# Sharing the band loads of a fused convolution and involution between two DMA queues

## The chip, the cores and the metric

The kernel runs on one core of a Trainium2 chip. Its engines work side by side, each through its own list of instructions in order: TensorE (PE in the profile) multiplies matrices into PSUM, VectorE (DVE) and ScalarE (ACT) do elementwise work, GpSimd (POOL) and SyncE (SP) here issue nearly all transfers. Engines wait for each other through semaphores. The metric is the device time of one execution in microseconds (us); lower is better.

## The reference

The input x has 32 images of 256 channels and 32 x 32 pixels. Two residual layers follow each other. `_gn` is a group norm over 32 groups of 8 channels.

```python
# layer 0: a 3x3 convolution, 256 to 256 channels, values clipped to the range of a 16-bit float
x = x + _L0_conv_ref(_gn(x), L0_conv_weight, L0_conv_bias)
# layer 1: an involution; n is _gn(x)
y = relu(batchnorm(einsum('oc,bchw->bohw', w1, n)))            # 256 -> 64 channels
w = einsum('oc,bchw->bohw', w2, y) + b2                        # 64 -> 16 groups x 49 taps, for each pixel
patches = [pad(n)[:, :, i:i+56, j:j+56] for the 49 taps]       # here 32 for 56
x = x + einsum('bgkhw,bgckhw->bgchw', w, patches)              # each pixel has its own 7x7 kernel for each group
```

In the second layer, each pixel thus has its own weights: 49 taps for each of 16 groups, shared by the 16 channels of a group.

## The kernel before

All images go through one software pipeline, written out by hand: the loop at lines 532 to 574 runs over steps, 16 per image, and in each step appends a few instructions for several images at once. `due(n, lag)` tells which image and which of its 16 steps stand at that point for a given lag. The order of a list of instructions of an engine is the order in which these calls are made. Nothing is reordered later.

For an image the work goes as follows.

- `front` (L272) normalizes x, runs the convolution (L318, tile `pc`), adds it to x (L334), normalizes again into `xn`, forms y (L366, L373) and the transposed pixels (L381, L385). It starts 58 steps ahead of the image's sums. x itself is loaded by SyncE (`load_x`, L103) 63 steps ahead, into one of five tiles; a tile is free when the image that held it has been stored.
- `weights` (L388) makes the per-pixel weights of four image rows with TensorE (L396, tile `pw`), and VectorE writes them with bias into the tile `w_sb` (L414). This tile is a ring of 24 image rows, which is three bands of eight rows. A slot may be overwritten when the scatter that read it has landed. It runs 18 steps ahead.
- `scatter` (L452) writes the weights of a band to a tensor `wd` in the chip's HBM memory, with seven transfers of SyncE (L463), 160 KB each. The rearrangement between weights per pixel and weights per tap lies in the addresses of this write and of the read that follows.
- `load_bands` (L465) reads a band of eight rows back into one of three band tiles. It takes 16 transfers, each of which fills 8 of the 128 partitions with 8 x 2 rows of 4496 bytes. All of them are issued by GpSimd (L475). A band has to wait for its scatter, and for TensorE to have finished with the band three before it.
- `sums` (L486) multiplies a band with the pixels (L500, tile `acc`), twice per band, and `add_windows` (L508) adds the result to x (L516). `store` (L518) sends half an image out by SyncE (L521).

There are four bands per image, so 128 bands, 2048 band loads and 896 scatters in an execution. `scatter` of band k+1 comes at the same step as, and in the list ahead of, `load_bands` of band k, for most k; the two stores, the load of x for a later image and the first scatter of the next follow at an image's end.

The tile framework gives the transfers of each kind of queue eight semaphores in turn: eight for GpSimd's queue and eight for the others. A transfer waits for the one eight before it on the same set. So eight of GpSimd's transfers and eight of SyncE's can be under way. GpSimd does nothing else in the body than issue band loads.

Of the kernel before, what the change touches and what calls it, by code (L numbers as in the profile page):

```python
# [40 lines left out]
JC = W // SIDES  # L41
# [9 lines left out]
WB = G * WIN  # L51
WPIX = K1 * WB + XR
# [6 lines left out]
ROW = S * WPIX  # L59
WR = 4  # L60
NBAND = 3
NPIX = 6
RING = 24
FRONT = -58
# [5 lines left out]
def tile_quant_conv_then_involution(  # L70
# [16 lines left out]
    nc = tc.nc  # L87
# [56 lines left out]
    y_sb = [const.tile([P, N // 2], F32, name=f"y_{i}") for i in range(2)]  # L144
    bands = [const.tile([P, SIDES, WINC * WB + XR], F32, name=f"band_{i}") for i in range(NBAND)]
    for t in bands[CH:]:
        nc.gpsimd.memset(t, 0.0)
    pixels = [const.tile([P, 2, PAIRS, PAIR], F32, name=f"pixels_{i}") for i in range(NPIX)]
    for t in pixels:
# [41 lines left out]
    for col, cols, at, n in (  # L191
# [8 lines left out]
        )  # L200
        nc.sync.dma_start(to, bands[NBAND - 1][:H, 0, :n].unsqueeze(1).to_broadcast([H, cols, n]))

# [69 lines left out]
    def front(b):  # L272
# [103 lines left out]
        for m in range(0, M, 2):  # L376
            yield
            pt = ps_m.tile([P, 2, C], F32, tag="m", name="pt")
            for i in range(2):
                for h in range(CH):  # L380
                    nc.tensor.transpose(  # L381
                        pt[:, i, h * P : (h + 1) * P], xn[:, h, (m + i) * P : (m + i + 1) * P], ident
                    )
            to = pixels[(b * M + m) // 2 % NPIX].rearrange("p i a (v c) -> p (i a) v c", c=GC)
            nc.scalar.copy(to[:, :, ::2], pt.rearrange("p i (a v c) -> p (i a) v c", v=2, c=GC))  # L385
# [79 lines left out]
    def load_bands(b, k):  # L465

        band = bands[(b * K + k) % NBAND]
        for i in range(JC):
            j = i // 2 + i % 2 * JC // 2
            src = bass.AP(  # L470
                tensor=wd.tensor,
                offset=wd.offset + k * TR * ROW + (j + PAD1) * WPIX,
                ap=[[ROW - 1, TR], [JC * WPIX, SIDES], [1, WPIX]],
            )
            nc.gpsimd.dma_start(band[j::JC, :, j * WB : j * WB + WPIX], src)  # L475

    def windows(b, m):

# [7 lines left out]
    def sums(b, m):  # L486

        k, d = divmod(m, SIDES)
        j0 = 0 if d else PAD1
        band = bands[(b * K + k) % NBAND][:, d]  # L490
        px = pixels[(b * K + k) % NPIX][:, d]
        for h in range(CH):
# [34 lines left out]
    def due(n, lag):  # L527

        b, i = divmod(n - lag, per)
        return (b, i) if 0 <= b < B else (None, None)  # L530

    with tc.manual_schedule():
        fronts = {}
        for n in range(FRONT, B * per + 2):
            b, i = due(n, FRONT)
# [10 lines left out]
            b, i = due(n, 0)  # L546
            if b is not None and i % 2 == 0:
                sums(b, i // 2)
            b, i = due(n, 1)
# [6 lines left out]
            b, i = due(n, 2)  # L556
            if b is not None and i == 2 * (M - 1 - SIDES):
                store(b, 0)
            b, i = due(n, -LEAD)
# [3 lines left out]
            b, i = due(n, -LEAD + 1)  # L563
# [4 lines left out]
            b, i = due(n, LOAD)  # L568
            if i == 0 and b > 0:
                x_tiles[b] = load_x(b)  # L570

            b, i = due(n, 3 - 4 * NBAND)
            if b is not None and i % 4 == 0:
                load_bands(b, i // 4)
# [37 lines left out]
```

## Time and profile before

| what | value |
|---|---|
| time, median of 3 runs | 1547.64 us (1541.66 to 1551.72) |
| profiled execution | 1520.43 us, span 1518.7 us |
| TensorE busy | 1317.0 us, 87% |
| GpSimd busy | 1141.8 us, 75% |
| VectorE busy | 865.6 us, 57% |
| ScalarE busy | 741.9 us, 49% |
| moved by DMA | 369.36 MB, 243 GB/s in the mean |
| GpSimd's queue (q0) | 147.59 MB, 35.7% of the 16 engines' span |
| SyncE's queue (q1) | 217.29 MB, 48.7% |
| band load, issue to landing | median 4.6 us |
| scatter transfer, issue to landing | median 5.4 us |

Busy shares are means over a start of about 80 us in which no bands are loaded, a long body, and a tail of some 110 us in which no new image comes in. A queue's share of the DMA engines is the time that its packets took, divided by sixteen times the span. An engine's idle time is listed by what ended it, with the total, the number of times and the longest one.

### The profile page before, as it was taken

Reading aid. Unit: us, or ns where it says so; the run is one execution under the profiler, and the core shown is the slowest. Engines: PE = TensorE matmul, PEld = TensorE weight load, DVE = VectorE, ACT = ScalarE, POOL = GpSimd, SP = SyncE. Lnnn points to the kernel's source line nnn. Section 1 sums busy time; section 2 is a strip of 40 time slices with the busy share of each in tenths; the row PEclk is TensorE's granted clock in tenths of the full one; section 3 lists DMA queues with packets and bytes.
Section 4 is the critical chain, followed back from the end, with each engine's and each line's share of the span. In section 5 each row is a group of like instructions: output and inputs, shape, how many; then the busy total and the mean of one; then the engine's idle time right before and its main releaser. Section 6 shows DMA issues by size and latency. Waiting matters only on the chain.

```text
span 1518.7 us, 70106 instructions
## 1 busy us (share of the span) xinstructions
PE 1317.0 (87%) x29760; PEld 865.2 (57%) x29760; DVE 865.6 (57%) x2764; ACT 741.9 (49%) x1699; POOL 1141.8 (75%) x2068
## 2 busy tenths in 40 slices
PE   5899989989998988989989898998989887998664
PEld 2456656656566555656656565665656565665543
DVE  4356656656665654656656565565656555665442
ACT  5665545435555544555545455554545554553200
POOL 6068787778777787877877777778777787788786
PEclk9899999999999999999999999999999999999877
DMA  6088998988998898898989898989989888988885
GB/s 198 5 232 248 265 256 254 270 255 243 267 252 246 257 270 258 236 273 240 258 245 272 247 259 241 258 259 255 280 248 264 239 251 238 272 250 238 250 232 149
DMA packets 372375, 369.36 MB, mean 243 GB/s; under 512 B 84768, under 2 KB 314336, under 8 KB 371808
## 3 DMA queue, kind: packets, MB, share of 16 engines
q1 hardware_dynamic: 273760, 217.29, 48.7%
q0 software_dynamic: 98304, 147.59, 35.7%
q8 instruction: 236, 3.87, 1.0%
q14 instruction: 75, 0.61, 0.1%
HBM read 183.81 MB, written 180.74 MB: 240 GB/s over the span
## 4 chain that ended last, share of the span: by engine, by line
PE 43%; DMA 29%; POOL 12%; issue 7%; DVE 4%; ACT 3%; SPq 2%; POOLq 0%; DVEq 0%; ACTq 0%
DMA band<-wd 24%; PE pc L318 17%; PE acc L500 13%; POOL band L475 12%; PE pw L396 8%; DMA wd<-w_sb 5%; DVE w_sb L414 2%; PE pt L381 2%; PE py L366 2%; SPq L463 2%; PE pg L221 1%; ACT junk L213 1%; ACT y L373 1%; DVE x L516 1%; DVE w_sb L154 0%
## 5 line engine op out<-in xcount | busy, mean ns | idle before, releaser
L475 POOL DMA_DIRECT2D band<-wd x2048 | 1117.1, 548 | 362.8 <-DMA band<-wd 218.1
L414 DVE TENSOR_TENSOR w_sb<-pw,b_sb 128x16 f32<-128x16 f32 (+9 forms) x1920 | 453.8, 349 | 569.7 <-PE pw L396 567.8
L318 PE MATMUL pc<-xq,wq 128*128 128x496 f16 (+3 forms) x2304 | 543.5, 383 | 11.3 <-ACT xq L266 5.9
L500 PE MATMUL acc<-band,pixels 64*32 64x190 f32 (+1 forms) x16384 | 420.7, 327 | 93.6 <-DMA band<-wd 78.8
L500 PEld LDWEIGHTS acc<-band,pixels 64*32 64x32 f32 x16384 | 306.1, 109 | 165.4 <-issue 93.5
L318 PEld LDWEIGHTS <-wq 128*128 128x128 f16 x2304 | 208.7, 99 | 312.5 <-issue 111.0
L396 PE MATMUL pw<-w_sb,y 64*32 64x224 f32 (+1 forms) x8192 | 295.8, 337 | 23.4 <-issue 22.7
L516 DVE TENSOR_TENSOR x<-acc,x 128x380 f32<-128x380 f32 (+1 forms) x512 | 263.4, 515 | 39.2 <-PE acc L500 30.2
L396 PEld LDWEIGHTS pw<-w_sb,y 64*32 64x32 f32 x8192 | 186.9, 108 | 50.0 <-issue 35.6
L213 ACT ACTIVATE junk<-x 128x512 f16<-128x512 f32 (+1 forms) x192 | 148.0, 771 | 137.3 <-DVE r L244 120.0
L385 ACT COPY pixels<-pt 128x512 f32<-128x512 f32 x128 | 74.4, 581 | 244.3 <-PE pt L381 244.3
L213 ACT ACTIVATE junk<-x,mean 128x1024 f16<-128x1024 f32 x128 | 147.1, 1149 | 4.1
L381 PE MATMUL pt<-ident,xn 128*128 128x128 f32 x512 | 81.1, 281 | 25.3 <-ACT ve L240 15.2
L332 DVE TENSOR_SCALAR q<-pc 128x512 f16<-128x512 f32 x128 | 87.3, 682 | 25.1 <-PE pc L318 25.1
L266 ACT ACTIVATE xn<-x,off,rstd 128x512 f32<-128x512 f32 x128 | 96.1, 799 | 0.0
L334 DVE SCALAR_TENSOR_TENSOR x<-q,bias_sb,x 128x512 f32<-128x512 f16 x128 | 91.9, 718 | 0.4
L221 PEld LDWEIGHTS pg<-sums,avg 128*128 128x128 f32 x320 | 54.0, 194 | 56.5 <-ACT y L373 30.6
L381 PEld LDWEIGHTS pt<-ident,xn 128*128 128x128 f32 x512 | 59.0, 142 | 44.2 <-ACT ve L240 18.3
L266 ACT ACTIVATE xq<-x,off,rstd 128x1024 f16<-128x1024 f32 x64 | 78.6, 1233 | 9.0 <-PE pc L318 8.4
L221 PE MATMUL pg<-sums,avg 128*128 128x2 f32 x320 | 47.6, 232 | 37.5 <-ACT y L373 22.0
L228 ACT ACTIVATE mean<-pg 128x2 f32<-128x2 f32 x64 | 11.0, 171 | 133.6 <-PE pg L221 133.6
L366 PEld LDWEIGHTS py<-xn,w_sb 128*64 128x64 f32 x2048 | 64.8, 142 | 19.6 <-issue 9.3
(39 smaller groups left out, 375.7 us busy)
## 6 DMA issues: line engine op xcount, KB each, us to landing
band<-wd POOLq DMA_DIRECT2D x2048, 70.2 KB, 4.6
wd<-w_sb SPq DMA_DIRECT2D x896, 160.0 KB, 5.4
x<-in_x SPq DMA_DIRECT2D x64, 512.0 KB, 5.9
out<-x SPq DMA_DIRECT2D x64, 512.0 KB, 6.3
band<-in_w SPq DMA_DIRECT2D x2, 1152.0 KB, 8.2
w_sb<-in_w SPq DMA_DIRECT2D x2, 196.0 KB, 9.8
wd<-band SPq DMA_DIRECT2D x2, 180.0 KB, 3.9
b_sb<-in_b SPq DMA_DIRECT2D x7, 14.0 KB, 8.0
```

The source lines that it names most:

```text
L213: nc.scalar.activation(junk[:, n0:n1], src[:, h, n0:n1], func, bias=bias, accum_out=self.sums[:, part, h : h + 1])
L221: nc.tensor.matmul(pg[:, :CH], avg, self.sums[:, i, :], start=i == 0, stop=i == self.parts - 1)
L266: nc.scalar.activation(dst, src, AF.Identity, bias=self.off[:, one], scale=self.rstd[:, one])
L318: nc.tensor.matmul(pc.rearrange("p (r c) -> p r c", c=W)[:, r0 - nt * RT : r1 - nt * RT, c0:c1], wq[:, kh, k, mh * P : (mh + 1) * P], xq[: ...
L334: nc.vector.scalar_tensor_tensor(xt[:, mh, cols], q, bias_sb[:, mh : mh + 1], xt[:, mh, cols], ALU.add, ALU.add)
L366: nc.tensor.matmul(py[i * CR : (i + 1) * CR, cols], w1_sb[:, kh, :], px[:, r : r + 2], start=kh == 0, stop=kh == CH - 1,)
L381: nc.tensor.transpose(pt[:, i, h * P : (h + 1) * P], xn[:, h, (m + i) * P : (m + i + 1) * P], ident)
L396: nc.tensor.matmul(pws[i][t * TW : (t + 1) * TW, r, : dj.stop - dj.start], y_sb[b % 2][half, (r0 // 2 + r) * W : (r0 // 2 + r + 1) * W], w ...
L414: nc.vector.tensor_tensor(to, pws[i][:p, r : r + rows, e, d0 * G : d1 * G].rearrange("p r (d g) -> p r d g", g=G), b2_sb[:p, e, d0 * G : d ...
L475: nc.gpsimd.dma_start(band[j::JC, :, j * WB : j * WB + WPIX], src)
L500: nc.tensor.matmul(at[t * TW : (t + 1) * TW, h, :, f - top : l - top], px[p, a, v * GC : v * GC + TW], of[:, :, 2 * a + v, f - top : l - top],
L516: nc.vector.tensor_tensor(x_at, of, x_at, ALU.add)
```

## The change

Of the 16 transfers of a band, the fourth, eighth, twelfth and sixteenth are issued by SyncE, the other twelve by GpSimd as before. What is loaded, from where and to where stays as it is. It is meant to take issue work off GpSimd, using a queue that exists already.

```diff
 WR = 4
 NBAND = 3
+SHARE = 4
 NPIX = 6
...
                 ap=[[ROW - 1, TR], [JC * WPIX, SIDES], [1, WPIX]],
             )
-            nc.gpsimd.dma_start(band[j::JC, :, j * WB : j * WB + WPIX], src)
+            queue = nc.sync if i % SHARE == SHARE - 1 else nc.gpsimd
+            queue.dma_start(band[j::JC, :, j * WB : j * WB + WPIX], src)
```

In the changed program SyncE's list per image holds 28 scatters, 2 stores, 2 loads of x and 16 band loads, in the order: seven scatters of band k+1, four loads of band k. One store stands ahead of the last of an image's four scatter groups and the other right behind it; four band loads follow that second store, and the two loads of x come after them. TensorE's first matmul of a band now waits for twelve semaphores of transfers where it waited for eight.

## The prediction

> **What bounds the kernel now.** I read the chain of waits on the page first, since it says which work follows which to the end, then the costliest groups, then who waits for whom, and last the stages.
>
> ```profile
> PE 43%; DMA 29%; POOL 12%; issue 7%; DVE 4%; ACT 3%; SPq 2%; POOLq 0%; DVEq 0%; ACTq 0%
> DMA band<-wd 24%; PE pc L318 17%; PE acc L500 13%; POOL band L475 12%; PE pw L396 8%; DMA wd<-w_sb 5%; DVE w_sb L414 2%; PE pt L381 2%; PE py L366 2%; SPq L463 2%; PE pg L221 1%; ACT junk L213 1%; ACT y L373 1%; DVE x L516 1%; DVE w_sb L154 0%
> ```
>
> The band loads hold 24% + 12% = 36% of the chain, in flight or being issued. TensorE holds 43%, so there are two streams of nearly equal weight. The groups show what a load costs its issuer:
>
> ```profile
> L475 POOL DMA_DIRECT2D band<-wd x2048 | 1117.1, 548 | 362.8 <-DMA band<-wd 218.1
> L500 PE MATMUL acc<-band,pixels 64*32 64x190 f32 (+1 forms) x16384 | 420.7, 327 | 93.6 <-DMA band<-wd 78.8
> ```
>
> GpSimd issues 2048 loads at 548 ns, 1117 us. Who waits for whom:
>
> ```profile
> POOL band L475 <- DMA band<-wd: 218.1, 271, 3.2
> POOL band L475 <- DMA wd<-w_sb: 72.9, 31, 56.1
> POOL band L475 <- issue: 52.9, 70, 3.3
> POOL band L475 <- PE acc L500: 2.1, 6, 0.5
> PE acc L500 <- DMA band<-wd: 78.8, 42, 5.5
> PE pw L396 <- issue: 22.7, 13, 4.1
> ```
>
> GpSimd waits 218 us for its own loads: each load waits for the one eight before it. It waits for TensorE to free a band for only 2 us, and for scattered weights for 73 us, 56 of them before the first image. So from 83 us to 1506 us (1423 us) GpSimd is busy (1117) or held by its own loads (218) or by small issue gaps (53): 1388 us, 98%. It is a full queue. The landings in the trace agree: over images 3 to 28 the first L500 matmul of a band follows the band's last landing by 0.1 us in the median for the first of an image's four bands, and its first load starts 4.9 to 12.5 us after the band buffer was free. Bands arrive just in time.
>
> ```profile
> 110.00:1403.00 1293.00, 1168.38 (x26987) 769.50 (x26970) 770.04 (x2496) 661.07 (x1518) 1006.97 (x1847) 0.98 0.90 255
> 1403.00:1485.00 82.00, 52.51 (x1498) 40.78 (x1505) 38.24 (x139) 12.27 (x26) 66.28 (x123) 0.82 0.86 242
> 1485.00:1519.00 34.00, 14.95 (x432) 11.05 (x422) 8.28 (x16) 0.00 (x0) 20.06 (x37) 0.75 0.44 126
> ```
>
> In these stages (columns: length, busy PE, PEld, DVE, ACT, POOL, clock, DMA share, GB/s) TensorE is 90% busy until 1403 us, and only 67 of 116 us after that, when no new image feeds it. So the loads cost little in the body and much in the tail. Gaps of TensorE over 1 us that end at L500 add up to about 42 us after 1403 us; the other 37 or so of the 79 lie in the body, 1.2 us per image of 44.3 us.
>
> **What the Trainium skill says.** "DMA: Bandwidth & Descriptors", section "Issuing engines are not separate DMA queues": transfers of all issuers run on the same 16 DMA engines and interleave; several issuers save only issue time. Here issue time is what is full, 98% of GpSimd, and the two queues do share engines at a DMA share of 0.90, so I expect issue relief and no bandwidth. The same page, section "Why a DMA increments its semaphore by 16 and not by 1": a transfer uses the largest number up to 16 of engines that divides the slowest dimension of both sides, and a hardware queue takes the lowest-numbered ones, while GpSimd's goes round. A load here has 8 partitions and 8 rows, hence 8 engines, always the same half on SyncE's queue. No run so far shows that.
>
> **The change part by part.**
> *GpSimd.* 16 of 64 loads per image leave it: 512 x 0.548 = 281 us of issue, and with them about a quarter of the 218 us, some 54 us. A band needs 12 x 0.548 = 6.6 us plus about 1.3 us of waits, 8 us, against 8.8 + 2.1 = 10.9 now and a pace of 44.3 / 4 = 11.1 us. GpSimd stops being full; it will wait for scattered weights and freed bands instead, which come 4 to 12 us before it uses them now.
> *SyncE, cost of a load.* Its issue of this shape isn't in the trace. Nearest rows: the scatter of L463 at 302 ns at least, 678 median, 2247 at most, and the x load at about 0.53 us. I take 0.75 us, because the four stand right behind seven scatters; ends 0.3 and 1.5. 512 x 0.75 = 384 us, 12 per image.
> *SyncE, room.* Its own waits:
>
> ```profile
> SPq L463 <- DVE w_sb L414: 434.6, 122, 49.6
> SPq L103 <- DMA out<-x: 146.8, 27, 8.6
> SPq L463 <- DVE x L516: 57.5, 98, 2.0
> ```
>
> All its waits are near 700 us, 650 of them in the body: 20 us per image, so 12 us fit. 4.6 us of the 20 is the x load waiting for a store to land; by the order of the changed program four loads stand between that store and the x load, so these 3 us are hidden.
> *Waits added and what is queued behind.* The order on SyncE becomes: scatter of band k+1, loads of band k, with stores and x loads between. The loads wait for TensorE to free the band, which the scatter just ahead implies, since its weights come later in TensorE's order; I put that at nothing. They also share eight slots with the scatters. Behind the loads stand the next scatter, two stores and the x load. Following one image in the trace (690 to 736 us), SyncE idles 7.2, 3.5, 0.6 and 0.1 us ahead of the four scatters. Four loads (3 us) fit before the first two, and push the other two, a store and the x load by 2 to 4 us. Who feels it: VectorE, which overwrites a slot of w_sb once its scatter has landed. That slack, from landing to L414, is 0.2 to 9.1 us, median 4.3, for an image's first band, the late one, and median 5.4 or more for the others. And ScalarE, whose first read of x comes a median of about 5 us after landing. A delay of 3 us is mostly absorbed; I charge 0.3 us per image, 10 us, and 3 us for x.
> *TensorE.* Its wait for a band names 12 semaphores for 8: two more EVENT_SEMAPHORE of about 0.1 us each with the gap behind it, 128 x 0.2 = 26 us if exposed. When the band is early they run beside pc matmuls of L318 (as at 700 us), so I take 5.
> *Landing.* Same bytes, same engines: 0 for the mean. In packets the page gives band loads 35.7% of 16 engines; a quarter, 8.9 points, doubled on one half of the engines, makes 85.5 + 8.9 = 94% there and 77% on the other. Those shares count queueing: the median 4496-byte packet takes 174 ns, the mean 246, so true load is lower and I take no loss, with 0 to 60 us as bounds.
>
> **Sum.** Body: of 37 us of waits I recover 34. Tail: a band takes 9.2 us there; 12 loads make 7 us, and TensorE's 67 us in 12 bands are 5.6, so of 42 us about 28 come back. 62 - 10 - 3 - 5 = 44 us. 1547.6 - 44 = 1503.
>
> **Rivals.**
> 1. *TensorE's floor is reached*: all 79 + 4 us of band waits go and nothing new comes. For it: SyncE's 20 us of room. Against: the small slack of w_sb. 1548 - 83 = 1465; earlier bands don't help ScalarE's share of the waits. Chance 0.2.
> 2. *SyncE's queue takes the wait over*: scatters 4 to 5 us late, so that VectorE, then pw (L396), stall 2 us per image, 62 us, which cancels the gain: 1548. For it: L396 already has 23 us of gaps, at 333 us one of 4.1 us, with a scatter in flight for 8.2 us. Against: the slack above. Chance 0.11.
> 3. *Slower*: half of the DMA engines fill up, scatters land 6 us late and stall VectorE for 3 us per image: 93 + 18 - 62 = 49 us net, 1597; or with 1.5 us per load SyncE needs 24 us where 20 are free, some 2 us beyond what the x wait hides, 62 - 28 = 34 us more, 1582. For it: DMA share 0.90. Against: 243 GB/s are moved as before. Chance 0.12.
>
> **How the numbers follow.** My forecast, 1503, has 0.57. It spreads from 1490 to 1530, since the charges of 18 us may be as small as 4 or as large as 44, and all of that is faster by over 1% (below 1532). With rival 1 faster has 0.77, same 0.11 (rival 2), slower 0.12 (rival 3). The range goes from 1462, just under rival 1, to 1560, past rival 2, and leaves rival 3 out.
>
> **What will show it.** GpSimd: 1536 loads, about 841 us busy, waits that name wd<-w_sb or acc more than before. L500's wait for band<-wd under 35 us. The chain led by TensorE, with band loads under 20%. SyncE: waits for w_sb down from 435 to under 250 us. The last three bands closer than 9 us each. Wrong, if L396's gaps grow past 60 us, if SyncE's loads take over 1.2 us, or if scatters land over 8 us after issue in the median (5.4 now).

## The result and the profile after

The changed kernel takes 1481.45 us in the median of 4 runs (1477.42 to 1488.62); the kernel before took 1544.65 us beside it (1536.92 to 1551.72). The ratio is 0.9596, with a 95% interval of 0.9555 to 0.9638: about 63 us or 4% less. The forecast was 1503 us.

The kernel before runs at different speeds on different chips: on the four chips of the experiments below its median lies between 1522 and 1549 us, and its profile shown ahead is of an execution of 1520 us. Runs on different chips are therefore compared by their ratio to the kernel before on the same chip, and steps within the two profiles add up to 42 us (1518.7 to 1476.7 us), not to 63. Ratios use fast executions alone, which leaves out two of the four of e6 and one of the kernel before beside e1 to e4, and the time given for e6 is the median of its other two. Lines move by one or two in the changed file: L475 became L477, L500 L502, L463 L464, L414 L415, L396 L397.

The chain of waits on the page of the changed kernel, by engine and by line:

```profile
DMA 37%; PE 37%; SPq 9%; DVE 6%; POOL 5%; issue 4%; ACT 2%; DVEq 0%; POOLq 0%; ACTq 0%
DMA band<-wd 20%; DMA wd<-w_sb 16%; PE pc L319 14%; PE acc L502 12%; SPq L464 7%; PE pw L397 7%; POOL band L477 5%; DVE w_sb L415 3%; PE pt L382 2%; SPq L477 1%; DMA out<-x 1%; DVE x L518 1%; PE py L367 1%; ACT junk L214 1%; PE pg L222 1%
```

GpSimd's issue of loads has gone from 12% of the chain to 5%. But TensorE doesn't lead it. The scatters (wd<-w_sb) have risen from 5% to 16%, and SyncE's issue of them from 2% to 7%. The waits between engines say the same (columns: us in total, times, longest):

```profile
POOL band L477 <- DMA band<-wd: 399.1, 279, 9.3
POOL band L477 <- DMA wd<-w_sb: 112.5, 24, 54.5
...
DVE w_sb L415 <- DMA wd<-w_sb: 72.9, 20, 6.9
ACT junk L214 <- DMA x<-in_x: 65.4, 45, 3.0
...
DVE w_sb L415 <- DMA band<-wd: 36.5, 9, 6.3
...
PE acc L502 <- DMA band<-wd: 22.1, 29, 5.1
...
PE pw L397 <- DVE w_sb L415: 18.7, 25, 3.0
...
PE pw L397 <- issue: 17.0, 19, 2.5
```

The two that were next to nothing before, from the same view of the kernel before:

```profile
ACT junk L213 <- DMA x<-in_x: 4.3, 4, 2.5
...
DVE w_sb L414 <- DMA wd<-w_sb: 1.9, 1, 1.9
```

TensorE's wait for bands fell from 79 to 22 us. Two waits are new: VectorE waits for transfers before it may overwrite w_sb, 73 + 36 us where it was 1.9, and ScalarE waits for x, 65 us where it was 4.3. The 399 us of GpSimd look worse than the 218 before and aren't. Taken apart by the place in the band, GpSimd's gaps ahead of the first load of a band grew from 29 to 331 us, and the gaps ahead of all others fell from 273 to 210. It now waits to be allowed to begin. A band's first load waits for semaphores on which SyncE's scatters and SyncE's loads both count, so 226 of these 331 us stand under band<-wd. Its own full slots hold it less than before.

SyncE's own waits, those of over 20 us:

```profile
SPq L464 <- DVE w_sb L415: 71.9, 25, 47.9
SPq L104 <- DMA out<-x: 57.5, 27, 3.5
SPq L477 <- DMA wd<-w_sb: 31.4, 45, 1.9
SPq L477 <- DMA x<-in_x: 23.0, 21, 2.4
SPq L523 <- DVE x L518: 20.4, 16, 7.5
```

SyncE waited 435 us for weights before, and 72 us now, 48 of them before the first scatter. When it comes to a scatter, the weights have been ready for some time. In the trace, from the end of the last L415 that a scatter group stands behind to its first scatter, the medians of the four bands of an image are 5.6, 4.8, 2.1 and 4.4 us (images 3 to 28; negative numbers below mean a start shortly before that end). Before the change the scatter started at once (0.1 us at most). Between 200 and 1250 us SyncE issues transfers for 80% of the time, 55% before.

The stages of the changed kernel (length, busy PE, PEld, DVE, ACT, POOL, clock, DMA share, GB/s), cut to match those of before:

```profile
110.00:1363.00 1253.00, 1153.32 (x26718) 753.14 (x26721) 761.79 (x2474) 656.22 (x1513) 752.23 (x1375) 1.00 0.94 260
1363.00:1443.00 80.00, 60.48 (x1696) 41.11 (x1688) 45.57 (x157) 13.92 (x30) 52.48 (x96) 0.87 0.92 255
1443.00:1477.00 34.00, 17.08 (x495) 12.86 (x479) 8.38 (x16) 0.00 (x0) 15.29 (x28) 0.70 0.70 205
```

TensorE is 92% busy in the body (90% before), GpSimd 60% (78%). Measured by the first L502 matmul of each band, an image takes 43.71 us over the first 28 images where it took 44.54, 23 us in all. The 15 band steps after that take 9.51 us each where they took 10.58, 16 us in all. About 1.5 us come from an earlier start, and 1.3 us from what follows the last band's first matmul.

Not all of this is shorter waiting. Of the 42 us between the profiles, 37 are idle time of TensorE (201.7 us before, 164.7 after) and 5 are busy time (1317.0 and 1312.0 us). L318 and L500 together were busy for 964.2 us before and for 948.5 after, L396 for 295.8 and 300.0, and the granted clock in the body was 0.98 before and 1.00 after. Whether the clock is higher because TensorE waits less, or differs by itself between these executions, no run separates.

### The profile page after: what moved, and what is told of

The parts are those of the page before. It is cut to its first block, busy times and chain, and to the rows that moved or that the text cites. A ratio compares the mean times of both kernels' runs of the same rounds, so it can differ in the third digit from the quotient of the medians.

```text
span 1476.7 us, 70463 instructions
## 1 busy us (share of the span) xinstructions
PE 1312.0 (89%) x29760; PEld 850.6 (58%) x29760; DVE 865.6 (59%) x2764; ACT 738.7 (50%) x1699; POOL 865.1 (59%) x1556
## 3 DMA queue, kind: packets, MB, share of 16 engines
q0 software_dynamic: 73728, 110.69, 28.2%
## 4 chain that ended last, share of the span: by engine, by line
DMA 37%; PE 37%; SPq 9%; DVE 6%; POOL 5%; issue 4%; ACT 2%; DVEq 0%; POOLq 0%; ACTq 0%
DMA band<-wd 20%; DMA wd<-w_sb 16%; PE pc L319 14%; PE acc L502 12%; SPq L464 7%; PE pw L397 7%; POOL band L477 5%; DVE w_sb L415 3%; PE pt L382 2%; SPq L477 1%; DMA out<-x 1%; DVE x L518 1%; PE py L367 1%; ACT junk L214 1%; PE pg L222 1%
## 5 line engine op out<-in xcount | busy, mean ns | idle before, releaser
L477 POOL DMA_DIRECT2D band<-wd x1536 | 840.4, 549 | 599.2 <-DMA band<-wd 399.1
L415 DVE TENSOR_TENSOR w_sb<-pw,b_sb 128x16 f32<-128x16 f32 (+9 forms) x1920 | 455.6, 350 | 536.5 <-PE pw L397 427.0
L319 PE MATMUL pc<-xq,wq 128*128 128x496 f16 (+3 forms) x2304 | 537.7, 380 | 10.1 <-ACT xq L267 6.0
L502 PE MATMUL acc<-band,pixels 64*32 64x190 f32 (+1 forms) x16384 | 410.8, 321 | 45.5 <-DMA band<-wd 22.1
L502 PEld LDWEIGHTS acc<-band,pixels 64*32 64x32 f32 x16384 | 296.9, 107 | 118.9 <-issue 86.0
L397 PE MATMUL pw<-w_sb,y 64*32 64x224 f32 (+1 forms) x8192 | 300.0, 334 | 36.4 <-DVE w_sb L415 18.7
L397 PEld LDWEIGHTS pw<-w_sb,y 64*32 64x32 f32 x8192 | 181.2, 107 | 74.8 <-issue 50.7
L222 PEld LDWEIGHTS pg<-sums,avg 128*128 128x128 f32 x320 | 53.7, 193 | 57.2 <-ACT y L374 30.6
L222 PE MATMUL pg<-sums,avg 128*128 128x2 f32 x320 | 47.4, 232 | 37.4 <-ACT y L374 14.0
L367 PE MATMUL py<-xn,w_sb 128*64 128x64 f32 x2048 | 69.0, 227 | 6.4 <-ACT xn L267 5.5
```

The lines of the kernel that those rows point to most:

```text
L222: nc.tensor.matmul(pg[:, :CH], avg, self.sums[:, i, :], start=i == 0, stop=i == self.parts - 1)
L319: nc.tensor.matmul(pc.rearrange("p (r c) -> p r c", c=W)[:, r0 - nt * RT : r1 - nt * RT, c0:c1], wq[:, kh, k, mh * P : (mh + 1) * P], xq[: ...
L367: nc.tensor.matmul(py[i * CR : (i + 1) * CR, cols], w1_sb[:, kh, :], px[:, r : r + 2], start=kh == 0, stop=kh == CH - 1,)
L397: nc.tensor.matmul(pws[i][t * TW : (t + 1) * TW, r, : dj.stop - dj.start], y_sb[b % 2][half, (r0 // 2 + r) * W : (r0 // 2 + r + 1) * W], w ...
L415: nc.vector.tensor_tensor(to, pws[i][:p, r : r + rows, e, d0 * G : d1 * G].rearrange("p r (d g) -> p r d g", g=G), b2_sb[:p, e, d0 * G : d ...
L477: queue.dma_start(band[j::JC, :, j * WB : j * WB + WPIX], src)
```

## The experiments

The theory was: before the change GpSimd's list of loads is full and sets the pace; the change takes that limit away and fills SyncE's list instead, so that scatters are late. Its rivals: a gain in proportion to the issue time moved; SyncE's queue as such; the bytes; and, for what the change leaves on the table, the half of the DMA engines that SyncE's loads use. Results, with the ratio to the kernel before on the same chip:

| kernel | loads on SyncE, of 16 | time, us | ratio (95% interval) |
|---|---|---|---|
| before | 0 | 1522 to 1549 | 1 |
| e5 | 1 | 1475.68 | 0.9537 (0.9460 to 0.9613) |
| e1 | 2 | 1450.92 | 0.9380 (0.9331 to 0.9428) |
| e1 again (e11) | 2 | 1441.01 | 0.9450 (0.9410 to 0.9491) |
| e6 | 3 | 1451.31 | 0.9386 (0.9295 to 0.9478) |
| the change | 4 | 1481.45 | 0.9596 (0.9555 to 0.9638) |
| e2 | 8 | 1761.95 | 1.1393 (1.1331 to 1.1454) |
| e3, on ScalarE's queue | 0 | 1757.53 | 1.1374 (1.1285 to 1.1464) |
| e4, a quarter left out | 0 | 1443.54 | 0.9324 (0.9270 to 0.9377) |
| e10, small ones in their place | 0 | 1484.14 | 0.9727 (0.9665 to 0.9790) |
| e9, two and two small ones | 2 | 1454.67 | 0.9531 (0.9474 to 0.9588) |
| e9 again (e12) | 2 | 1453.31 | 0.9527 (0.9487 to 0.9567) |
| e7, stores and x on GpSimd | 4 | 1506.88 | 0.9751 (0.9687 to 0.9815) |
| e8, the same | 2 | 1526.76 | 0.9880 (0.9808 to 0.9951) |

**Other shares (e1, e2, e5, e6).**

```diff
-SHARE = 4
+SHARE = 8      # e1; 2 in e2, 16 in e5, 5 in e6
```

> Every eighth load on SyncE (2 of 16 per band) instead of every fourth. Theory A (GpSimd's full queue was the limit, and with a quarter moved SyncE's list has become the limit): GpSimd then needs 14 x 0.55 + about 1.5 us of waits = 9.3 us per band, still under the 10.9 us pace, and SyncE gets 8 loads x 0.73 = 6 us per image back, so the body is as fast as with a quarter or a little faster; time 1465 to 1490, VectorE's wait for wd<-w_sb down from 73 us to under 30. Theory B (the gain is in proportion to the issue time taken off GpSimd): half the gain, about 1513.

> Every second load on SyncE (8 of 16 per band). Theory A: SyncE needs about 25 us for scatters, stores and x, and 32 x 0.73 = 23 us for loads, 48 us per image, more than the 43.7 us of now, so SyncE sets the pace: 1570 to 1640, slower than before, with VectorE waiting for wd<-w_sb over 200 us. Theory B: more relief, more gain, 1420 to 1450.

> One load of 16 per band on SyncE. Theory A (GpSimd's full queue first, SyncE's full list after): GpSimd needs 15 x 0.55 + some 1.7 us of waits = 9.9 us per band against a floor of 42.3 / 4 = 10.6 us per band that the run with the quarter left out showed, so it is barely no longer the limit: 1455 to 1490. If the gain followed the issue time taken off in proportion, it would be a quarter of that with four loads moved away for nothing (1549 to 1444), about 1520.

> Three loads of 16 per band on SyncE (the fifth, tenth and fifteenth). Theory A: between the runs with two (1451) and four (1481), since SyncE's list fills up step by step: 1453 to 1472, with VectorE's wait for wd<-w_sb between 2 and 73 us.

One load moved brings as much as the change, within the intervals, two bring more than four, and eight make the kernel slower by 14%. A gain in proportion to the issue moved is out. e1 was forecast at 1465 us or more and took 1451. With three loads the ratio is that of e1, scatters start 1.2, -0.4, -0.4 and 0.8 us after their weights, and VectorE waits 2.4 us for transfers, so the lateness of the change sets in between three loads and four. The chain of waits with two loads is what the forecast expected of the change:

```profile
PE 70%; DMA 14%; issue 4%; POOL 4%; ACT 4%; DVE 3%; SPq 1%; POOLq 0%; DVEq 0%; ACTq 0%
```

TensorE holds 70% of it. Scatters start 1.2, -0.4, -0.4 and 0.4 us after their weights, nearly as before. Of the 64 us between the profiles of before and e1, 17 are TensorE's busy time (1317.0 to 1300.4 us, at a mean granted clock of 0.962 and 0.978); of these too no run tells the cause. With eight loads they start 7 to 13 us late, SyncE issues for 80% of the body, as in the change, and VectorE stands:

```profile
DVE w_sb L415 <- DMA band<-wd: 272.2, 42, 12.7
DVE w_sb L415 <- DMA wd<-w_sb: 211.9, 36, 10.8
```

Here 80% of issue is a full list: SyncE's waits for earlier transfers to land, ahead of loads and scatters, add up to 152 us (74 in the change), and semaphore instructions and small gaps stand between. The size was forecast too low: 1762 us against 1570 to 1640.

**A quarter left out (e4), and small transfers in its place (e10).**

```diff
-            queue = nc.sync if i % SHARE == SHARE - 1 else nc.gpsimd
-            queue.dma_start(band[j::JC, :, j * WB : j * WB + WPIX], src)
+            if i % SHARE < SHARE - 1:
+                nc.gpsimd.dma_start(band[j::JC, :, j * WB : j * WB + WPIX], src)
+            else:                                          # e10 alone
+                n = (b * K + k) * SHARE + i // SHARE
+                nc.gpsimd.dma_start(spare[n % (2 * SHARE)], bias0[:GN].unsqueeze(1))
```

> The quarter of the loads that the change moves is left out altogether: GpSimd issues 12 of 16 loads of a band, nobody the other four (their part of the band keeps what was there), so 37 MB less are moved. This is the floor of the change. Theory A: what the change pays for SyncE's four loads per band is seen as the difference: 1430 to 1455, body at about 42 us per image and tail at under 8.5 us per band. Theory D (TensorE's own list is the limit after the change, SyncE's loads cost nothing): 1470 to 1481.

> As the run in which a quarter of the loads was left out (1444), but GpSimd issues a transfer of 32 bytes in the place of each load left out; those four loads of a band are again not made. Bytes are those of that run, the number of GpSimd's transfers is that of before. Theory A (GpSimd's issue of 16 transfers per band is the limit before): nearly all of the gain is lost again, 1515 to 1550; GpSimd's waits for its own slots shrink a little, because the small transfers land sooner. Theory F (the bytes were the limit): 1440 to 1455.

In e4 the issue of these loads and their bytes are both gone, and nobody takes them over. The ratio is 0.932, as forecast. That is the floor of this kind of change; two loads on SyncE come within 0.6 to 1.3 points of it. In e10, GpSimd again issues 16 transfers per band and moves hardly more bytes than in e4, and 4.0 of the 6.8 points of gain are lost, by ratios from two chips. So the number of GpSimd's transfers, not their bytes, makes up about 60% of what the floor shows. The forecast of "nearly all" was too high: GpSimd's waits for its slots are shorter here, with small transfers among them and fewer bytes moved.

```profile
POOL band L478 <- DMA band<-wd: 153.5, 183, 2.9
...
PE acc L506 <- DMA band<-wd: 76.5, 37, 5.5
...
POOL spare L481 <- DMA spare<-in_bias: 31.3, 37, 1.9
```

GpSimd's are 185 us where they were 218 before. It is full in both: in e10 it issues for 82% of the body and its gaps take nearly all of the rest. TensorE waits for bands as long as before, 76.5 us where it was 78.8; in the change it waits 22.

**The quarter on ScalarE's queue (e3).**

```diff
-            queue = nc.sync if i % SHARE == SHARE - 1 else nc.gpsimd
+            queue = nc.scalar if i % SHARE == SHARE - 1 else nc.gpsimd
```

> The same quarter of the loads on ScalarE's queue instead of SyncE's. Theory A: SyncE's list is as free as before the change (about 20 us per image idle), GpSimd is as relieved as in the change; ScalarE is busy 50% and has room for 16 x 0.73 = 12 us per image, but its loads make it wait for freed bands, which may hold back its sums. 1450 to 1485, faster than the change if these waits are small. Theory B: same as the change, 1481. Theory C (what helps is SyncE's queue as such, not the relief of GpSimd): no gain, 1545.

GpSimd has as few loads as in the change, SyncE has none, and the kernel is 14% slower. ScalarE's own waits tell why:

```profile
ACT pixels L386 <- DMA band<-wd: 192.9, 32, 9.3
ACT xq L267 <- DMA band<-wd: 105.7, 22, 6.0
ACT y L374 <- DMA band<-wd: 101.4, 25, 7.9
```

These three sum to 400 us. ScalarE's operations stand behind loads that wait for a slot, a scatter or a freed band, and TensorE waits for ScalarE (123 us ahead of L222 for pixels alone). SyncE is not quite free, since ScalarE's loads share its eight semaphores: its scatters wait 290 us for earlier transfers to land. But the first scatter of a band starts at most 0.4 us late in the median, and VectorE waits for no transfer at L415, so this is not what costs the time. The forecast named ScalarE's wait and gave a time only for the case that it is small; none of the three theories came near.

**SyncE relieved of stores and x (e7, e8).**

```diff
-            nc.sync.dma_start(xt[:, h], x[b, h * P : (h + 1) * P])
+            (nc.sync if b < 4 else nc.gpsimd).dma_start(xt[:, h], x[b, h * P : (h + 1) * P])
...
-        nc.sync.dma_start(out[b]...)
+        nc.gpsimd.dma_start(out[b]...)
```

> A quarter of the loads on SyncE as in the change, but the stores, and the loads of x from the fifth image on, are issued by GpSimd instead of SyncE. SyncE's list loses 2 x 0.67 + 2 x 0.55 us and some 2 us of waiting for a store per image, 4.5 us of 43.7; which DMA engines the band loads run on stays as it is. Theory A (SyncE's list is what the change runs into): near the run with two loads, 1445 to 1468, scatters again start within about 1 us of their weights. Theory E (what the change runs into is the half of the DMA engines that SyncE's loads use): no gain, 1475 to 1490.

> Two loads of 16 per band on SyncE, and the stores and loads of x on GpSimd. Theory A: SyncE is now far from full, but at 1451 TensorE's own list already holds 70% of the chain and the floor is about 1444, so little is left: 1440 to 1455.

Both came out far slower than forecast and leave the question open. In e7 scatters are on time again (-0.4 us for three of the bands, 0.9 us for one), but GpSimd has got waits of its own:

```profile
POOL band L477 <- DMA x<-in_x: 93.4, 51, 3.6
...
POOL band L477 <- DMA out<-x: 66.6, 41, 5.1
POOL out L523 <- DVE x L518: 50.2, 19, 6.4
```

The large transfers hold GpSimd's slots, and the stores make it stand until VectorE has finished, with band loads behind them: 210 us, and 163 in e8. With two loads on SyncE and the stores left there (e11) these waits are 10 us. In e8 ScalarE also waits 133 us for x. That scatters are on time in e7, with all four loads still on SyncE, fits a lateness that comes from SyncE's list and not from where its loads run; but a slower kernel also leaves SyncE more room.

**Small transfers on SyncE (e9, e12), beside two loads (e11).** To fill SyncE's list without bytes:

```diff
-            queue = nc.sync if i % SHARE == SHARE - 1 else nc.gpsimd
+            queue = nc.sync if i % (2 * SHARE) == 2 * SHARE - 1 else nc.gpsimd
             queue.dma_start(band[j::JC, :, j * WB : j * WB + WPIX], src)
+            if i % (2 * SHARE) == SHARE - 1:
+                n = (b * K + k) * 2 + i // (2 * SHARE)
+                nc.sync.dma_start(spare[n % (2 * SHARE)], bias0[:GN].unsqueeze(1))
```

> Two loads of 16 per band on SyncE (1451 without more), plus two transfers of 32 bytes per band on SyncE at the places where the change has its other two loads. They cost SyncE's list an issue each (estimated 0.6 us, as the load of the small bn vectors at the start), and move nothing to speak of. Theory A (the change with four loads falls behind the run with two because SyncE's list is full): most of the gap to the change comes back, 1465 to 1485. Theory E (it falls behind because four loads put more bytes on one half of the DMA engines): 1449 to 1458, as with two loads alone.

> Two loads of 16 per band on SyncE once more, on the same chip as the next run, because the kernel before took 1522 us on the chip of the run with the small transfers and 1545 to 1549 us in the runs ahead of it, so that times of different calls cannot be set side by side to 1%. Ratio to before 0.935 to 0.945 if the ratio carries over from chip to chip.

> The same with two transfers of 32 bytes per band on SyncE. Theory A (a full list of SyncE costs time, whatever the bytes): 10 to 25 us above the run with two loads alone, ratio to before 0.948 to 0.960. Theory E (only bytes on one half of the DMA engines cost): within 5 us of it.

The time of e9, 1454.67 us, is one that theory E allowed, but it can't be set beside e1, since the kernel before took 1522 us on that chip; by its ratio e9 lies between e1 and the change. So both were run on one chip: 1441.01 us (1437.65 to 1448.48) with two loads alone, 1453.31 us (1448.85 to 1463.23) with two 32-byte transfers per band added. That is 12 us for transfers that move next to nothing, as theory A had it; the slowest run without them (1448.48) is faster than the fastest with them (1448.85). SyncE issues for 83% of the body with them and for 74% without. Scatters are as late as in the change: 5.2, 4.0, 2.1 and 4.3 us. The waits at w_sb, first with small transfers, then without:

```profile
DVE w_sb L416 <- DMA wd<-w_sb: 50.3, 18, 6.6
DVE w_sb L416 <- DMA band<-wd: 40.1, 10, 5.8
...
PE pw L398 <- DVE w_sb L416: 16.1, 27, 3.3
```

```profile
DVE w_sb L415 <- DMA wd<-w_sb: 1.3, 1, 1.3
```

TensorE's own wait at that line is 0.5 us without them. So a full list of SyncE makes scatters late and VectorE wait, even where what fills it moves next to nothing. Between the change and two loads lie 1.5 to 2.2 points, some 22 to 33 us; 12 of them are shown to come from two more transfers in the list, by their issue and the slots that they take together. For the rest there are the bytes of the two further loads on SyncE's queue, their place on 8 engines, or their longer issue. No run separates these.

## Why the prediction was right

The relief of GpSimd was foreseen, and it makes the gain. What takes over as the limit was not: the forecast had TensorE lead, and scatters of SyncE came late instead. That the sum came out so close is in part luck, since two of its terms were off in opposite directions.

- *GpSimd's list is full and is the limit.* Right. One load moved already gives 4.6%, a quarter left out 6.8%, and filling the places with small transfers takes 4.0 of these points back, while TensorE waits for bands as before. In the changed kernel GpSimd issues 1536 loads in 840 us (841 were forecast), and the gaps between loads of one band fell by 63 us (54 were forecast).
- *SyncE's price of a load, 0.75 us.* Right: 0.73 us in the mean of the body, 583 ns median and 567 at least.
- *SyncE's room.* "20 us per image, so 12 us fit" was right as a sum and misleading as a finding. The loads fit, but they used up the slack in which SyncE waited for weights, so all four scatters of an image come 2 to 6 us late, where the forecast had two of them late by 2 to 4 us.
- *The charge for that, 10 us for w_sb and 3 us for x.* VectorE's wait is 109 us and ScalarE's for x 65 us. Most of this doesn't reach TensorE: its wait of L397 for VectorE and "issue" is 36 us where it was 23, a growth of 13, and its matmuls there are busy for 4 us longer. The small-transfer pair gives 12 us for a list as full. The charge was close for TensorE, and the waits behind it were sized too small by several times.
- *The body, 34 us less charges of 18.* The profiles show 23 us where this makes 16.
- *The tail, 28 us.* This term failed: 16 us came. The step was "12 loads make 7 us", with GpSimd as the only limit. With 12 loads on GpSimd and none elsewhere (e4) the same 15 steps still take 8.67 us each, so most of what is missing isn't SyncE's; two loads on SyncE take 9.43 and 9.33 (e1, e11), four take 9.51. For a stretch of the tail SyncE does set the pace, with seven scatters, four loads and now and then a store. Its timeline there (start, length, engine, line) leaves no room:

```profile
1424.44 2.96 SPq L477 DMA_DIRECT2D band<-wd  x4
1427.77 4.69 SPq L464 DMA_DIRECT2D wd<-w_sb  x7
1432.56 4.05 SPq L477 DMA_DIRECT2D band<-wd  x4
1436.98 5.08 SPq L464 DMA_DIRECT2D wd<-w_sb  x7
1442.16 2.98 SPq L477 DMA_DIRECT2D band<-wd  x4
```

  Two bands take 17.7 us here (1424.44 to 1442.16), 8.9 us each, where 7 were forecast. After 1454 us SyncE has only the last loads and stores left, and the last steps between bands are still 9.6, 9.4 and 7.3 us. What holds a band above 7 us in e4 is open. The two errors of 7 and 12 us nearly cancel, by luck: 44 us forecast, 42 between the profiles. Against the timed medians, 63 us, the sum is low by a third. How much of that is the execution of 1520 us behind the profile of before is not resolved.
- *TensorE's semaphores.* There are 771 EVENT_SEMAPHORE at L502 where there were 515, two more per band as forecast. Its gaps of "issue" kind at L502 grew from 9.9 to 21.2 us, so the 5 us charged for them may be too low.
- *What would show it.* L502's wait under 35 us: 22. SyncE's wait for weights under 250 us: 72. L397's gaps under 60 us: 36. A chain led by TensorE with band loads under 20% did not come: DMA and TensorE have 37% each, and band loads 20%. It came with two loads in place of four. "The last three bands closer than 9 us each" did not come either, but for the last step. GpSimd's wait for acc didn't grow (2 us), and that for wd<-w_sb went from 73 to 113. SyncE's loads stayed far below 1.2 us; how long scatters take to land the profile of the changed kernel doesn't give.
- *Eight engines.* The Trainium skill's rule for the number of engines ("DMA: Bandwidth & Descriptors", section "Why a DMA increments its semaphore by 16 and not by 1") had no run behind it. The changed kernel's page counts packets per queue:

```profile
q1 hardware_dynamic: 286048, 254.14, 60.9%
q0 software_dynamic: 73728, 110.69, 28.2%
```

  SyncE's queue has 12288 packets more for 512 loads, 24 each: 16 rows of 4496 bytes and 8 packets of 4 bytes, which fits eight engines that each report their end. On GpSimd's queue a load has 48 packets (73728 / 1536), 32 of them of 4 bytes. Which eight engines they are, the trace doesn't tell.
- *The rivals.* The change did run into SyncE's list, by rival 2's mechanism, though at 13 us rather than 62. The 1.5 us per load of rival 3 did not occur. Rival 1 put TensorE's floor at 1465 us, with all 83 us of waits for bands gone. It lies lower: the ratios of two loads (0.938 and 0.945) and of the quarter left out (0.932) make 1449, 1460 and 1440 of the 1544.65 us. TensorE's busy time of 1300.4 us (e1) and 1295.7 (e4), where it was 1317.0, is part of that.

## What to carry to other kernels

A queue whose issues and own slot waits fill its engine's time is a limit even if its engine shows 75% busy; look at what ended its gaps, and whether work it waits for was ready long before. When work is moved to another queue, count that queue's list too, and move only as much as takes the first one just off the limit: here one of 16 transfers gave 4.6%, two gave 5.5 to 6.2%, four gave 4%, and eight cost 14%. An idle wait in a list is no free room if what stands behind it has a date: filling SyncE's waits for weights made the next scatters late, and the same four loads that gave 4% on SyncE's list cost 14% on ScalarE's, half idle as it was.

## What the runs showed that was not expected

On GpSimd's queue the bytes hardly count for the issuer: 541 ns in the median for 32 bytes (e10), 547 for the 70 KB of a band load before, 566 for 512 KB of x (e7); a store of 512 KB took 744 (e7). On SyncE the 32-byte transfer costs 465 ns in the median (e12), a band load 583 and a scatter of 256 rows 655, with single scatters up to 2133 (both in the change). What stands ahead counts there: of the four loads of a band in the change, the first two behind the scatters take 817 and 923 ns in the mean, the others 600 and 580, and the median of a load is 823 ns with two loads per band, 583 with four and 567 with eight. A wait can be charged to the wrong transfer where two kinds share semaphores: VectorE overwrites slots that scatters read, and still 36 us of its waits stand under band<-wd in the changed kernel.
